# Result rows moved from the GpSimd queue to the SyncE queue in the main loop, and a tail that begins with rounds and runs each gate's conv three ticks behind its loads

## The chip, the cores and the metric

The kernel runs on one core of one Trainium2 chip. The metric is the device time of one execution in microseconds (us), as the median of several runs. The engines are called by the profile's names: PE (TensorE matmul) and PEld (its weight loads), DVE (VectorE), ACT (ScalarE), POOL (GpSimd) and SP (SyncE). SP computes nothing in this kernel, it only issues DMA transfers; POOL computes and also issues transfers of its own.

## What is computed

Two layers work on x of shape (8, 8, 512, 512), each with a residual:

```python
x = x + _L0_conv_ref(_gn(x), ...)     # low modes of a 2-D FFT, mixed over channels, and back
x = x + _L1_conv_ref(_gn(x), ...)     # layer 1, below

# layer 1
grid = drive                           # = x, all 8 channels
for _ in range(15):                    # the map
    mapped = 3.9 * grid * (1.0 - grid)
    local = conv3x3(mapped, K_local, groups=8)
    grid = 0.85 * (0.7 * mapped + 0.3 * local) + 0.15 * drive
cml_out = clip(grid, 0.0001, 0.9999)
nca_out = sigmoid(conv1x1(relu(conv3x3(x, Wp, bp)), Wu, bu))   # 8 -> 128 -> 8
gin = concat([x, cml_out, nca_out])                            # 24 channels
g = sigmoid(conv1x1(relu(conv3x3(gin, Wg1, bg1)), Wg2, bg2))
return g * cml_out + (1.0 - g) * nca_out
```

`_gn` is a group normalisation over pairs of channels. Everything is float32.

## The kernel before

One image of the batch is called an element; there are eight. For each element four kinds of work exist. Their only links are through planes in device memory (xn, the normalised input; cml, the map's result; nca, the result of the hidden branch) and through the order of each engine's instructions.

- **Layer 0** (`layer0`, the spectral pieces) loads x planes of the next element, computes, and writes xn.
- **The map** (`Slabs`, `Tail`, `Phase`) runs 15 steps on slabs of 32 rows that stay in SBUF: `convolve` (192 matmuls in the trace, L524) on PE, `settle` (L537 on DVE, L543 square on ACT), then `renew` (L570, L571), in which POOL issues small transfers that exchange edge rows between slabs. `drive` (L516, on POOL) prepares the summands; `load` (L495, on SP) fetches the slices dE and dO; `leave` stores cml (L600, on SP).
- **The hidden branch** (`Hidden`) works in 128 rounds of four rows per element. `round` makes 24 matmuls in the trace (L723) from a tile "cols", of which two exist; each serves four rounds. When the last round of a tile has been issued (`i == 3`), the tile after the next is requested (`self.load()`, L706, on SP). Every second round a `point` (L742) follows. After every fourth round, the sigmoid result y (L755 on ACT, one buffer) is stored to nca (L758). That is the store of **result rows**. The statement is put off with `later(1, store)` to the end of the tick, and it also sets `e.rows`, the number of rows of nca that gates may read.
- **The gates** (`Gate`) work in 43 blocks of 12 rows per element, on the element before the one that is mapped. `load` issues six transfers on SP (L778 three times: gin from xn, cml and nca; L783 three times: mix). `conv` (L793) follows in a later tick, `point` (L810) in the tick after that, and the output is stored in the next tick by SP (L828), which waits for DVE (L821).

All of this is written out as straight code, and `keep_order` binds each engine to the order of the source. The unit of the order is a **tick** (`turn`, `work`): up to two map steps, then `transfers` (the gates' loads by `others.feed`, and the map's loads), then up to two rounds, then one gate conv (`others.gate`), the hidden point, and one gate point (`others.point`). At the end of a tick the work that was put off is issued. So on SP a tick's gate loads stand ahead of a cols load that the rounds of the same tick request. A cols load that a later tick requests stands behind all of them.

`others.limit` is the number of gates that may be loaded and not yet convolved: two in the main loop, four in the tail. A gate can be convolved when the tick of its loads (`at`) is before the present one.

The last element has no successor. Its map runs with 56 of its 128 rounds (`ROUNDS_LAST`). The other 72 rounds and all 43 of its gates come after the map, in the loop from L1101 on, which is called **the tail** here. (The class `Tail` is something else, the last slab of the map.) In the tail before the change, a quota spreads the 72 rounds evenly over 39 ticks: one in tick 0, one in tick 1, two in most of the later ones. Tick 0 feeds four gates, tick 1 convolves the first of them.

Of the kernel before, what the change touches and what calls it, by code (L numbers as in the profile page):

```python
# [43 lines left out]
N = 512  # L44
# [8 lines left out]
GR = 12  # L53
ROUNDS, ROUNDS_LAST, FIRST_ROUNDS = 128, 56, 8
# [57 lines left out]
def view(t, offset, dims):  # L112

    return bass.AP(tensor=t.tensor, offset=t.offset + offset, ap=[list(d) for d in dims])
# [3 lines left out]
def conv_layers(ctx: ExitStack, tc: tile.TileContext, a, out):  # L118
    nc = tc.nc
# [9 lines left out]
    class Slots:  # L129
# [4 lines left out]
        def __init__(self, most):  # L134
            self.most, self.held = most, {}
# [26 lines left out]
    put_off, now = [], [0]  # L162

    def later(ticks, work):
        put_off.append((now[0] + ticks, work))
# [529 lines left out]
    class Hidden:  # L695
# [42 lines left out]
        def point(self, ps):  # L738

            for r, h in self.hs:  # L740
                for g in range(4):
                    nc.tensor.matmul(  # L742
                        ps[32 * g : 32 * g + 32], w_u[:, r % 4], h[:, g],
                        start=(r == self.hs[0][0]), stop=(r == self.hs[-1][0]),
                        tile_position=(0, 32 * g),
                    )
            if self.hs[0][0] % 4 == 0:
                self.y = wk.tile([P, N], F32, tag="y", name="y", bufs=1)
                nc.scalar.copy(self.y, ps)  # L749
            else:  # L750
                nc.vector.tensor_tensor(self.y, self.y, ps, ALU.add)  # L751
            self.hs.clear()
            if r % 4 == 3:
                y, r0 = self.y, 4 * (r - 3)
                nc.scalar.activation(y, y, AF.Sigmoid, bias=b_u)  # L755

                def store():
                    nc.gpsimd.dma_start(  # L758
                        out=view(self.e.nca, (1 + r0) * C * N, [[N, P], [1, N]]), in_=y
                    )  # L760
                    self.e.rows = r0 + 16

                later(1, store)
# [129 lines left out]
    class Others:  # L893


        def __init__(self):
            self.before, self.after, self.limit = None, None, 2
            self.mapped, self.paused, self.closed = deque(), False, False
            self.loaded, self.convolved, self.pointed = deque(), deque(), deque()
            self.longs = 0  # L900
# [42 lines left out]

        def gate(self, ps):
            self.longs = 0
            if not (self.loaded and self.loaded[0].at < now[0]):
                return False
            g = self.loaded.popleft()
            g.conv(ps)
            g.at = now[0]  # L950
            self.convolved.append(g)
            return True
# [28 lines left out]
    def element(b):  # L981
        e = Element(b)
        phase(e.halves[0])
        phase(e.halves[1] + [e.tail])
        elements.append(e)
        return e

    e = element(0)
# [3 lines left out]
    others = Others()  # L992
# [54 lines left out]
    def turn(at, rounds, e, after, t):  # L1047


        now_phases = [p for p in phases if at < p.end + 2]  # L1050

        def transfers():
            others.feed(t)
            for p in now_phases:
                p.fetch(at)

        def squares():
            for p in now_phases:
                p.squares(at)

        for p in now_phases:
            p.prepare(at)
        steps = [slots[i] for i in (at, at + 1) if 0 <= i < len(slots)]
        work(steps, rounds, e, after and after.hidden, transfers, squares)
# [4 lines left out]
    for b in range(B):  # L1069
        e = elements[b]  # L1070
        after = element(b + 1) if b + 1 < B else None
        others.after = after
        done, rounds = e.hidden.n, ROUNDS if after else ROUNDS_LAST
        first, second = phases[2 * b : 2 * b + 2]
        ticks = (second.end - at + 1) // 2
# [8 lines left out]
        for t in range(ticks):  # L1084
# [7 lines left out]
            more = done + quota[t] - e.hidden.n  # L1092
# [5 lines left out]
        others.mapped.append(e)  # L1098


    others.after, others.limit, others.paused, others.closed = None, 4, False, False  # L1101
    shared.most = SLOTS
    done, ticks = e.hidden.n, -(-N // GR) - 4
    for t in count():
        if e.hidden.n == ROUNDS and not others.mapped and not others.busy():
            break
        more = min(ROUNDS, done + (t + 1) * (ROUNDS - done) // ticks) - e.hidden.n
        turn(at, min(more, 2 - e.hidden.n % 2), e, None, GATES_FROM)
        at += 2
    tick(end=True)  # L1110
# [55 lines left out]
```

## Time and profile before

| what | value |
|---|---|
| median of 3 runs | 9497.11 us (9489.37 to 9503.13) |
| the profiled execution | time 9518.56 us, span 9516.7 us from first to last instruction |
| PE busy | 9080.2 us, 95% of the span |
| ACT, DVE, POOL busy | 4072.7, 5655.6, 3505.6 us |
| result stores L758 on POOL | 256, mean some 0.62 us of issue, 3.7 us to landing (median) |
| idle time of POOL before L758, waiting for y (ACT L755) | 373.5 us, 72 times |
| the map's last matmul (L524) ends | 9052 us |
| the tail, to the end of the span | from 9058 to 9516.7 us |

How to read it: the profiled execution is one single execution and slower than the median of the runs by some 21 us, so a sum of its parts is compared with its own time, and only differences are carried over to the median. A time in square brackets on a line of the timeline is the idle time of that engine before the instruction, with what ended it. A name like `gin<-nca` says what is written from what. "SPq" is SP's queue of DMA issues. The line of an issue gives only the time of issuing; when a transfer lands is seen from who waits for it.

### The profile page before, as it was taken

How to read it: one execution, taken by the hardware profiler on the slowest of the kernel's cores; microseconds unless marked ns; L12 is line 12 of the kernel's file. 1: busy time of each engine (PE TensorE's matmuls, PEld its weight loads, DVE VectorE, ACT ScalarE, POOL GpSimd, SP SyncE). 2: the span in 40 equal slices, each digit the busy share in tenths (PEclk: the TensorE clock that was granted, in tenths of full speed). 3: DMA queues.
4: the chain of work that ended last, by engine and by line, in shares of the span. 5: the costliest groups of instructions: out<-in, count | busy, mean ns of one | idle time of the engine just before them, and what ended most of it. 6: DMA issues, size and time to landing. Idle time of an engine off the chain costs nothing. (4 is left out here: it accounts for less than half of the span.)

```text
span 9516.7 us, 331665 instructions
## 1 busy us (share of the span) xinstructions
PE 9080.2 (95%) x148976; PEld 4064.1 (43%) x148976; DVE 5655.6 (59%) x5820; ACT 4072.7 (43%) x4285; POOL 3505.6 (37%) x4678
## 2 busy tenths in 40 slices
PE   6999999999999999999999999999999999999989
PEld 3444444444444444444444444444444444334433
DVE  5665566655666556665566555665556655555555
ACT  2444444444444444444344444444444444334422
POOL 3242434334343343433434333343433434343422
PEclk9999999999999999999999999999999999999999
DMA  4241365565655656655556556565565555565488
GB/s 150 83 127 35 94 170 131 144 145 136 156 134 146 139 133 154 162 137 139 136 143 160 137 126 157 128 164 138 125 161 138 160 135 119 142 151 126 104 210 201
DMA packets 682173, 1327.07 MB, mean 139 GB/s; under 512 B 146938, under 2 KB 152442, under 8 KB 653266
## 3 DMA queue, kind: packets, MB, share of 16 engines
q1 hardware_dynamic: 557568, 1181.97, 49.9%
q0 software_dynamic: 120832, 122.73, 4.8%
q8 instruction: 1171, 19.19, 0.9%
q14 instruction: 248, 2.03, 0.1%
q10 hardware_dynamic: 2354, 1.14, 0.0%
HBM read 977.48 MB, written 270.61 MB: 131 GB/s over the span
## 5 line engine op out<-in xcount | busy, mean ns | idle before, releaser
L524 PE MATMUL pair<-m,band 32*32 32x512 f32 x103680 | 3722.9, 605 | 184.6 <-issue 123.5
L543 ACT ACTIVATE m<-m 128x1024 f32<-128x1024 f32 x2016 | 2125.9, 1055 | 2500.1 <-DVE m L537 2419.2
L723 PE MATMUL pair<-cols,w_p 32*128 32x511 f32 (+1 forms) x24576 | 2867.6, 605 | 44.6 <-DVE m L537 20.9
L524 PEld LDWEIGHTS pair<-m,band 32*32 32x32 f32 x103680 | 1994.1, 103 | 1837.9 <-issue 1082.2
L570 POOL DMA_DIRECT2D m<-m x1568 | 862.7, 550 | 3591.7 <-ACT m L543 3519.7
L537 DVE SCALAR_TENSOR_TENSOR m<-pair,dO 128x1024 f32<-128x1024 f32 x1152 | 1356.2, 1219 | 1183.2 <-PE pair L524 1031.0
L723 PEld LDWEIGHTS pair<-cols,w_p 32*128 32x128 f32 x24576 | 1305.2, 187 | 1628.3 <-issue 1164.4
L537 DVE SCALAR_TENSOR_TENSOR m<-pair,dE 128x1024 f32<-128x1024 f32 x1008 | 1187.3, 1219 | 1105.3 <-PE pair L524 940.1
L731 DVE TENSOR_SCALAR h<-pair,b_p 128x1024 f32<-128x1024 f32 x1024 | 1311.2, 1282 | 868.5 <-PE pair L723 863.6
L729 ACT ACTIVATE h<-pair,b_p 128x1024 f32<-128x1024 f32 x1024 | 1140.4, 1114 | 916.8 <-PE pair L723 916.7
L742 PE MATMUL pair<-h,w_u 128*32 128x512 f32 x8192 | 1059.1, 610 | 34.5 <-ACT h L729 30.5
L793 PE MATMUL pair<-gin,w_g 128*32 128x511 f32 (+1 forms) x8256 | 963.4, 598 | 35.4 <-DMA gin<-nca 31.8
L816 POOL TENSOR_TENSOR mix<-mix 96x512 f32<-96x512 f32 x344 | 438.4, 1274 | 1273.8 <-ACT mix L814 1233.7
L571 POOL DMA_DIRECT2D m<-m x1568 | 844.1, 538 | 26.6 <-issue 23.2
L742 PEld LDWEIGHTS pair<-h,w_u 128*32 128x32 f32 x8192 | 245.4, 110 | 691.3 <-issue 353.6
L755 ACT ACTIVATE y<-y,b_u 128x512 f32<-128x512 f32 x256 | 184.8, 722 | 831.0 <-DVE y L751 831.0
L793 PEld LDWEIGHTS pair<-gin,w_g 128*32 128x32 f32 x8256 | 235.2, 110 | 713.0 <-issue 490.2
L798 POOL TENSOR_TENSOR mix<-mix 96x512 f32<-96x512 f32 x344 | 445.3, 1294 | 51.2 <-DMA mix<-cml 28.5
L547 POOL TENSOR_SCALAR dO<-dO 128x2048 f32<-128x2048 f32 x72 | 391.7, 5440 | 99.1 <-DVE m L537 98.0
L749 ACT COPY y<-pair 128x512 f32<-128x512 f32 x256 | 150.0, 586 | 646.0 <-PE pair L742 522.7
L821 DVE SCALAR_TENSOR_TENSOR mix<-mix,back 96x512 f32<-96x512 f32 x344 | 334.9, 974 | 143.9 <-POOL mix L816 143.9
L803 DVE TENSOR_SCALAR mix<-pair,b_g 128x512 f32<-128x512 f32 x344 | 257.7, 749 | 201.5 <-PE pair L793 200.3
(90 smaller groups left out, 3430.8 us busy)
## 6 DMA issues: line engine op xcount, KB each, us to landing
gin<-xn SPq DMA_DIRECT2D x344, 384.0 KB
cols<-xn SPq DMA_DIRECT2D x256, 512.0 KB
x<-in_x SPq DMA_DIRECT2D x120, 1024.0 KB
gin<-cml SPq DMA_DIRECT2D x344, 320.0 KB
gin<-nca SPq DMA_DIRECT2D x344, 320.0 KB
dE<-xn SPq DMA_DIRECT2D x288, 256.0 KB
dO<-xn SPq DMA_DIRECT2D x288, 256.0 KB
mix<-xn SPq DMA_DIRECT2D x344, 192.0 KB
```

Of the source, the lines that this page charges most:

```text
L524: nc.tensor.matmul(ps[h // 2][32 * t : 32 * t + 32, h % 2], band[at, self.channel(step - 1, h, t), dx], m[at, t, dx : dx + N], start=(n == ...
L537: nc.vector.scalar_tensor_tensor(u[:, at], ps[q], FLOOR, d[:, at], ALU.max, ALU.add)
L543: nc.scalar.square(u[:, at], u[:, at])
L570: nc.gpsimd.dma_start(out=view(tb, rb, dims), in_=view(ta, ra, dims))
L571: nc.gpsimd.dma_start(out=view(ta, ra + s, dims), in_=view(tb, rb + s, dims))
L723: nc.tensor.matmul(ps[g // 2][:, g % 2, lo:hi], w_p[p, dx, i % 2], self.cols[p, i // 2, at : at + hi - lo], start=(n == 0), stop=(n == 2), ...
L729: nc.scalar.activation(h[:, :2], ps[0], AF.Relu, bias=b_p)
L731: nc.vector.tensor_scalar(h[:, 2:], ps[1], b_p, 0.0, ALU.add, ALU.max)
L742: nc.tensor.matmul(ps[32 * g : 32 * g + 32], w_u[:, r % 4], h[:, g], start=(r == self.hs[0][0]), stop=(r == self.hs[-1][0]), tile_position ...
L793: nc.tensor.matmul(ps[32 * j : 32 * j + 32, lo:hi], gband[:, dx], gin[:, j, at : at + hi - lo], start=(n == 0), stop=(n == 2), tile_positi ...
L798: nc.gpsimd.tensor_tensor(d, d, ng, ALU.subtract)
L816: nc.gpsimd.tensor_tensor(d, d, mix[: GR * C, 2], ALU.mult)
```

## The change

The change has three parts.

1. The result store L758 is issued by SP instead of POOL as long as `others.lag` is 0, which is the whole time before the tail; in the tail POOL issues it as before. The last store ahead of the tail belongs to the first group.
2. A new number `others.lag` is 0 in the main loop and 2 in the tail. A gate can be convolved when `at + lag` is before the present tick: in the tail three ticks after its loads instead of one.
3. The tail's quota begins with two rounds in each of ticks 0 to 3. The 64 others are spread evenly over ticks 4 to 40 (before: all 72 over ticks 0 to 38). Since a tick takes no more than two rounds, and one after an odd number, five pairs of ticks with a single round each remain (before: two such pairs, apart from ticks 0 and 1).

The first gate's conv so moves from tick 1 to tick 3, the last one's from tick 43 to tick 45. The number of instructions of every kind stays the same.

```diff
                 def store():
-                    nc.gpsimd.dma_start(
+                    (nc.gpsimd if others.lag else nc.sync).dma_start(
                         out=view(self.e.nca, (1 + r0) * C * N, [[N, P], [1, N]]), in_=y
                     )
                     self.e.rows = r0 + 16
...
-            self.before, self.after, self.limit = None, None, 2
+            self.before, self.after, self.limit, self.lag = None, None, 2, 0
...
-            if not (self.loaded and self.loaded[0].at < now[0]):
+            if not (self.loaded and self.loaded[0].at + self.lag < now[0]):
                 return False
...
-    others.after, others.limit, others.paused, others.closed = None, 4, False, False
+    others.after, others.limit, others.lag = None, 4, 2
+    others.paused, others.closed = False, False
     shared.most = SLOTS
-    done, ticks = e.hidden.n, -(-N // GR) - 4
+    done, ticks = e.hidden.n, -(-N // GR) - 2
     for t in count():
         if e.hidden.n == ROUNDS and not others.mapped and not others.busy():
             break
-        more = min(ROUNDS, done + (t + 1) * (ROUNDS - done) // ticks) - e.hidden.n
+        more = min(ROUNDS, done + 8 + (t - 3) * (ROUNDS - done - 8) // (ticks - 4)) - e.hidden.n
+        if t < 4:
+            more = 2
         turn(at, min(more, 2 - e.hidden.n % 2), e, None, GATES_FROM)
```

## The prediction

> **What bounds the kernel now.** I read the page's busy table first, then busy time by stretch over the whole span, then the timeline of the last 480 us, then the waits. The busy table says which engine to follow.
>
> ```profile
> PE 9080.2 (95%) x148976; PEld 4064.1 (43%) x148976; DVE 5655.6 (59%) x5820; ACT 4072.7 (43%) x4285; POOL 3505.6 (37%) x4678
> ```
>
> PE is busy 95% of 9516.7 us. By stretch (length, busy us of PE, PEld, DVE, ACT and POOL, clock, DMA share, GB/s) the end reads:
>
> ```profile
> 9042.00:9093.00 51.00, 27.00 (x350) 10.67 (x344) 18.89 (x17) 5.18 (x5) 2.34 (x2) 0.77 0.70 173
> 9093.00:9478.00 385.00, 385.00 (x3405) 137.00 (x3404) 223.73 (x200) 124.53 (x144) 104.33 (x94) 1.00 0.88 218
> 9478.00:9517.00 39.00, 15.49 (x112) 4.01 (x105) 14.63 (x16) 3.42 (x5) 14.09 (x10) 0.83 0.52 129
> ```
>
> The tail's middle is PE without a gap; its start holds one hole. The timeline shows the hole and what SP does in it:
>
> ```profile
> 9058.34 5.43 PE L723 MATMUL pair<-cols,w_p 32*128 32x512 f32 x48
> 9064.38 8.32 SPq L778 DMA_DIRECT2D gin<-xn  x1
> 9087.05 4.53 PE L793 MATMUL pair<-gin,w_g 128*32 128x512 f32 x24 [23.28 <-DMA gin<-nca]
> 9104.80 0.32 SPq L778 DMA_DIRECT2D gin<-xn  x1
> 9112.47 0.38 SPq L706 DMA_DIRECT2D cols<-xn  x1
> 9115.29 0.32 SPq L778 DMA_DIRECT2D gin<-xn  x1
> ```
>
> PE runs two rounds, then idles 23.28 us until the first gate's loads land. SP issues four gates' loads (24 transfers) from 9064.38 to 9104.42, then gate 5's, and only then, at 9112.47, the next rows for the rounds (cols). For the main loop the waits matter (total us, times, longest):
>
> ```profile
> POOL nca L758 <- ACT y L755: 373.5, 72, 28.5
> SPq L828 <- DVE mix L821: 3294.1, 303, 29.4
> ACT y L749 <- DMA nca<-y: 59.4, 14, 5.3
> ```
>
> POOL stands in front of the result store; SP has much idle time; the one buffer y is hardly ever late (13 of those 14 waits are in the tail).
>
> **What the Trainium skill says.** "DMA: Bandwidth & Descriptors", section Queues, rings and completion order: a sequencer's DMA is split over rings of its own row, and each DMA engine consumes a ring in order. The trace agrees: SP lets a transfer go when the one eight places before it has landed (gate 6's first load goes at 9115.29, as gate 5's first, issued 9104.80, lands), so landings keep nearly the order of issue. The same page, section Issuing engines are not separate DMA queues: another issuing engine saves only the issue time. The trace gives that time, 0.62 us a store on POOL. "TensorE: Matmul & The Clock Gate", section Part 1: The HAM clock gate: after an idle window the array runs at half rate. Agreed: granted clock 0.50 from 9068 to 9086, and the gate conv after the hole takes 4.53 us where later ones take 2.78.
>
> **The tail, step by step.** A full tick (two rounds, their point, a gate's conv and point) repeats every 10.63 us (9093.23, 9103.86 and on). Two ticks of one round each take 14.41 (9210.19 to 9224.60): one gate more, so a gate costs 3.78 and two rounds with their point 6.85. Two rounds and point without a gate take 7.84 (164.90 to 172.74 to 180.58 at the kernel's start), since the point then waits for h.
> Before: the tick of rounds 58 and 59 starts at 9093.23. From there 70 rounds (35 x 6.85) and 37 gates (37 x 3.78) give 9472.9; the last round's tick does end at 9473.0. The remaining 43.8 us, five gates that wait for loads, are alike after the change: there too gates 39 to 43 remain when rounds end, and gate 42 waits for the last store.
> After: ticks 0 to 3 run rounds 56 to 63. They take 3 x 7.84, then 6.85 plus gate 1's conv 2.78: 9058.34 + 33.2 = 9091.5. Gate 1's loads landed at 9087, so its conv no longer waits. The 23.3 us hole is filled.
> **What is late next:** tick 4 begins with round 64, whose cols tile is loaded when round 59 is issued, in tick 1. But tick 0's feed has put four gates' loads ahead of it in SP's queue. It can take gate 5's place, 9104.80. That place landed after 10.5 us; the cols transfer of before (512 KB) took 11.1, its landing read from the store that SP lets go eight transfers later. So 9115.6, plus about 1.2 us since two result stores of 256 KB now fall before it and only one did (256 KB at 218 GB/s). PE resumes at 9117 after 25 idle us, cold: the first two rounds at 141.8 took 8.32 instead of 5.43, a cold gate conv 1.75 more; I take 2.3. Then 64 rounds (32 x 6.85 = 219.2) and 37 gates (139.9): 9478.4. Against 9472.9 the tail is **5.5 us longer**. One hole has replaced another of the same size. Bounds: if cols were in time, 9091.5 + 359.1 = 9450.6, -22; if it lands at 9121, as late as the slowest nearby transfer (13 us), +10.
> The later single rounds of the new schedule (five pairs of ticks instead of two) cost no PE work. They need loads sooner: 359.1/37 = 9.7 us a gate; gates 2 to 6 landed every 7.8 to 9.6, so they are covered, by 12 to 17 us of slack between landing and conv in steady state.
>
> **The stores in the main loop.** 237 of 256 stores lie before 9042, and they plus one more go to SP.
> *Off POOL:* 237 x 0.62 = 147 us of issue and 558 us of standing. Behind a store stands next a renewal (L570) in 165 cases, always with a gap, since it waits for ACT's square of the next tick, later in ACT's order than y; removing the store does nothing there. In 44 cases drives (L516) or L547 follow at once, 20 of these chains hold a renewal, and all PE waits on m<-m at a matmul sum to 28.4 us. I take -3 us; bounds 0 and -20.
> *Onto SP:* 237 x 0.62 us. Matching each store's place in program order to SP's transfers: in 189 places SP sits idle across it. In 48 the next transfers move back, together 141 us, of which 131 in 30 places, at most 7.6. Queued behind it are dE/dO slices, x planes and gate loads; after each such run SP idles 7 to 29 us, so no delay is carried on. At 2834.5 the dO slices land 7.6 late, 2852; the drive (2.7) ends 2855, its reader starts 2858.8: hidden. At 2367.4 a gate's loads land 6 late, about 2390, when its conv starts (2390.19): just covered. I take +2; bounds 0 and +44 (a third of 131).
> *The buffer y:* a store on SP's rings lands behind loads of up to 14 us, where POOL's took 3.6 in the middle. In 16 places it would land after the next copy (L749) wants y, together 42 us; ACT idles some 3.8 us before its next square, which covers most. I take +2; bounds 0 and +20.
>
> **Sum.** +5.5 - 3 + 2 + 2 = +6.5 us. The profiled execution has span 9516.7 and time 9518.6, 21.5 above the median 9497.1; the difference carries over: 9497.1 + 6.5 = 9503.6, told as **9503**.
>
> **Rivals.**
> A, the forecast (0.61): hole for hole, main loop neutral; 9503, own range 9489 to 9516. For it: the queue order and the landing times.
> B, the hole is really filled (0.19): cols lands in time, or POOL's relief is worth its bound; -22 - 3 gives 9472, and part of it up to 9485. Against it: 24 transfers of 6.4 MB stand ahead, from 9072.7 on, and at the tail's 218 GB/s they need 30 us, till 9103.
> C, slower (0.20): the store at the head of SP's queue waits for y and holds dE/dO and gate loads whose landing PE needs; a third of 131 us plus the tail's 5.5 gives 9546. It decides as soon as the slack between a load's landing and its reader is under the delay, as it nearly is at 2390. Half of its weight lies under 9530.
> The change not doing what it says is not likely: the lag only delays convs that are ready, but tick 1 to 3 have rounds in their place.
>
> **How the numbers follow.** What a measurement tells from no change is about 0.2%, 19 us: faster is below 9478, slower above 9516. B gives faster 0.19, C slower 0.20, A the same 0.61. The range 9474 to 9530 holds A, most of B and half of C; it takes in the tail's bounds (-22, +10) and most of the main loop's.
>
> **What would show it.** Right: no wait at the first L793 of the tail; a PE wait on cols<-xn of 22 to 28 us before round 64; cold matmuls after it; the tail from 9058 to the last round's end 3 to 8 us longer; L758 on SP, POOL's wait on L755 gone but in the tail; PE idle from 400 to 9042 within 15 us of the 300 us that busy time by stretch gives there. Wrong: round 64 starting near 9092; PE waits on dO, gin or m<-m in the main loop growing by over 20 us.

## The result and the profile after

| kernel | runs | median, us | ratio to before, 95% interval |
|---|---|---|---|
| before | 6 | 9505.62 (9489.37 to 9530.28) | |
| changed | 6 | 9443.68 (9431.73 to 9457.31) | 0.9932 [0.9916, 0.9949] |
| changed, once more, beside the last experiments | 6 | 9440.28 (9422.39 to 9465.90) | 0.9945 [0.9925, 0.9965] |

The change is worth 0.55 to 0.7%, 52 to 65 us. The forecast was 9503, no change. The page of the changed kernel, for comparison with the busy table of before:

```profile
span 9440.3 us, 331607 instructions
PE 9039.4 (96%) x148976; PEld 4068.9 (43%) x148976; DVE 5657.6 (60%) x5820; ACT 4072.3 (43%) x4285; POOL 3367.1 (36%) x4440
q0 software_dynamic: 101792, 60.33, 3.1%
q8 instruction: 1171, 19.19, 0.9%
```

POOL has lost 238 instructions: the stores are gone from it. PE has as many instructions as before but is busy 41 us less, so its matmuls ran at full clock for longer. The line q8 (packets, MB, share of 16 engines) was passed over in the prediction; it becomes the main point below.

**The tail grew.** From its first round to the end of the span it took 9516.7 - 9058.34 = 458.4 us before and 9440.3 - 8974.16 = 466.1 after: 7.7 us more; to the end of the last round, which is what the forecast of 5.5 us sums, it is 415.2 against 425.5 us, 10.3 more (the second trace of the changed kernel, experiment 12, has 420.2, 5.0 more). The timeline of the changed kernel's tail:

```profile
8974.16 5.43 PE L723 MATMUL pair<-cols,w_p 32*128 32x512 f32 x48
8978.59 7.74 SPq L758 DMA_DIRECT2D nca<-y  x1
8995.73 0.58 ACT L749 COPY y<-pair 128x512 f32<-128x512 f32 x1 [14.94 <-DMA nca<-y]
8996.37 4.46 PE L723 MATMUL pair<-cols,w_p 32*128 32x512 f32 x24 [11.45 <-ACT y L749]
9016.46 2.78 PE L793 MATMUL pair<-gin,w_g 128*32 128x512 f32 x24
9020.36 1.01 SPq L706 DMA_DIRECT2D cols<-xn  x2
9032.81 5.01 PE L723 MATMUL pair<-cols,w_p 32*128 32x512 f32 x24 [11.86 <-DMA cols<-xn]
9355.06 6.89 PE L723 MATMUL pair<-cols,w_p 32*128 32x512 f32 x48 [3.17 <-DMA cols<-xn]
```

The first gate's conv (9016.46) no longer waits. In place of its 23.28 us there are two waits, 11.45 and 11.86. The second is the forecast one, for cols behind 24 gate loads. The first wasn't foreseen: the last store before the tail still goes to SP, stands there behind the cml stores, and holds the one buffer y. PE comes 11 us later to round 64, so it waits so much less there: the forecast's 25 us are the sum, 23.3, in two pieces. A third wait, of 3.17 us at 9355.06, is again for cols; the forecast had none there.

**The gain lies in the main loop.** Between the first and the last convolve (L524) before took 8871.5 us and after 8784.0, 87.5 less. By stretch (length, busy us of PE, PEld, DVE, ACT, POOL, clock, DMA share, GB/s), first of before, then of after:

```profile
400.00:9042.00 8642.00, 8341.87 (x140604) 3757.86 (x140581) 5150.76 (x5217) 3801.03 (x3970) 3263.57 (x4314) 0.98 0.55 137
```

```profile
400.00:8960.00 8560.00, 8297.28 (x140688) 3764.14 (x140672) 5158.45 (x5218) 3799.86 (x3970) 3130.82 (x4085) 0.99 0.56 138
```

PE's idle time falls from 300.1 to 262.7 us and its clock rises. The waits say which idle time. Of before (us in total, times, longest):

```profile
PE pair L524 <- issue: 123.5, 79, 4.1
PE pair L524 <- DMA m<-m: 28.4, 17, 3.8
```

Of after, with SP's wait at the store and the y buffer:

```profile
PE pair L524 <- issue: 103.3, 69, 3.9
PE pair L524 <- DMA m<-m: 22.7, 13, 4.2
SPq L758 <- ACT y L755: 922.1, 187, 10.1
ACT y L749 <- DMA nca<-y: 44.9, 10, 14.9
```

The largest loss on PE has no releaser ("issue"), and it shrinks. SP now stands 922 us before the store, and no group of PE's waits in the main loop of this trace is longer by more than 4.2 us. Of ACT's 44.9 us for y, 2.6 lie in the main loop (at 2345.0 and 6943.3), the rest in the tail.

### The profile page after: what moved, and what is told of

It is laid out like the page before. It is cut to its first block, busy times and chain, and to the rows that moved or that the text cites. A ratio compares the mean times of both kernels' runs of the same rounds, so it can differ in the third digit from the quotient of the medians.

```text
span 9440.3 us, 331607 instructions
## 1 busy us (share of the span) xinstructions
PE 9039.4 (96%) x148976; PEld 4068.9 (43%) x148976; DVE 5657.6 (60%) x5820; ACT 4072.3 (43%) x4285; POOL 3367.1 (36%) x4440
## 3 DMA queue, kind: packets, MB, share of 16 engines
q8 instruction: 1171, 19.19, 0.9%
## 5 line engine op out<-in xcount | busy, mean ns | idle before, releaser
L524 PE MATMUL pair<-m,band 32*32 32x512 f32 x103680 | 3703.2, 604 | 159.3 <-issue 103.3
L524 PEld LDWEIGHTS pair<-m,band 32*32 32x32 f32 x103680 | 1997.7, 103 | 1788.1 <-issue 997.9
L793 PE MATMUL pair<-gin,w_g 128*32 128x511 f32 (+1 forms) x8256 | 962.2, 598 | 11.3 <-DMA gin<-nca 7.9
L793 PEld LDWEIGHTS pair<-gin,w_g 128*32 128x32 f32 x8256 | 235.3, 110 | 686.8 <-issue 462.9
L516 POOL TENSOR_SCALAR dO<-dO,base 128x512 f32<-128x512 f32 x288 | 208.8, 735 | 574.6 <-DMA dO<-xn 532.7
```

Source lines behind the costliest of these rows:

```text
L524: nc.tensor.matmul(ps[h // 2][32 * t : 32 * t + 32, h % 2], band[at, self.channel(step - 1, h, t), dx], m[at, t, dx : dx + N], start=(n == ...
L793: nc.tensor.matmul(ps[32 * j : 32 * j + 32, lo:hi], gband[:, dx], gin[:, j, at : at + hi - lo], start=(n == 0), stop=(n == 2), tile_positi ...
```

## What "issue" is: the place at 2371 us

The convolve that starts at 2371.11 before starts at 2361.62 after. Before:

```profile
2366.84 0.38 SPq L706 DMA_DIRECT2D cols<-xn  x1
2367.40 0.33 SPq L778 DMA_DIRECT2D gin<-xn  x1
2369.55 0.44 SPq L783 DMA_DIRECT2D mix<-nca  x1
2371.11 5.76 PE L524 MATMUL pair<-m,band 32*32 32x512 f32 x167
2371.99 0.36 SPq L182 DMA_DIRECT2D x<-in_x  x1
2373.05 0.60 POOL L758 DMA_DIRECT2D nca<-y  x1 [2.87 <-ACT y L755]
2380.98 2.00 PE L524 MATMUL pair<-m,band 32*32 32x512 f32 x25 [4.10 <-issue]
```

After:

```profile
2357.35 0.38 SPq L706 DMA_DIRECT2D cols<-xn  x1
2361.62 6.58 PE L524 MATMUL pair<-m,band 32*32 32x512 f32 x192
2363.23 0.33 SPq L758 DMA_DIRECT2D nca<-y  x1
2363.73 0.51 SPq L778 DMA_DIRECT2D gin<-xn  x1
2366.08 0.42 SPq L783 DMA_DIRECT2D mix<-nca  x1
2368.13 5.43 PE L723 MATMUL pair<-cols,w_p 32*128 32x512 f32 x48
```

Before, SP issues a gate's six loads from 2367.40 on, ahead of the convolve. The convolve stops after 167 of its 192 matmuls for 4.10 us, and the profile names nothing that it waited for. In the changed kernel the store stands in front of those loads on SP and waits for y; the loads leave 6 us later relative to PE's work, and the convolve runs through.

What PE waits for is in the trace's DMA records: the queue q8 carries packets of 16 KB, 1171 in all, one for some 254 of PE's 297,952 instructions (19.19 MB in the page). The Trainium skill ("Advanced Engine Details and Errata", section ISA Cache) says that instructions are cached in lines of 16 KB, 256 instructions; the packets agree. What follows is read from these records; no line of the page has it. At this place the packet that follows the convolve's start begins 1.1 us after it in the changed kernel and 6.8 us after it before; it takes 1.1 to 1.3 us, and PE resumes 1.8 us after it has landed. What the DMA engines moved between the convolve's start and the packet's shows why SP's wait matters here (length, busy us of PE, PEld, DVE, ACT, POOL, clock, DMA share, GB/s), of before and of after:

```profile
2371.11:2377.89 6.78, 5.77 (x171) 3.25 (x167) 3.24 (x4) 2.70 (x3) 0.60 (x1) 1.00 1.07 191
```

```profile
2361.62:2362.74 1.12, 1.12 (x40) 0.50 (x39) 0.83 (x2) 0.26 (x1) 0.00 (x0) 1.00 0.06 22
```

Before, 191 GB/s go on for 6.78 us until the packet begins; after, SP stands at the store, the data pause at 22 GB/s, and the packet begins in the pause.

The same pattern of late packets is found all over the main loop: from 400 us on, before had 58 gaps of over 0.6 us ahead of L524 without a releaser, 115.1 us together. All 58 end 1.23 to 1.78 us after such a packet has landed (median 1.42), and in the 4 us before them the core's DMA moved 222 GB/s (median), against 137 over the stretch. PE waits for its own instructions, which come late in bursts of loads. A burst is needed, but isn't enough: of the 1107 such packets from 400 us to the last convolve of before, 566 began when less than 160 GB/s had landed in the 4 us ahead, and none of them was followed (1 to 2 us after it landed) by a stop of PE over 0.6 us without a releaser; of the 443 that began after 190 GB/s or more, 60 were. What makes these 60 late and not the others is not shown.

A stop costs twice. The Trainium skill ("TensorE: Matmul & The Clock Gate", Part 1) says that the array's clock is halved after at least one idle window of about 3.4 us. Here shorter stops were followed by half clock too: of the 65 stretches at a granted clock of 0.5 in the main loop of before, 51 had no single gap as long as that from 8 us ahead of their start to 4 us behind it. Half of PE's busy time in such stretches, which is what the slow clock costs, is 143.6 us before and 102.6 (54 stretches) after. The 87.5 us so divide into gaps 37.6 (304.7 to 267.1), cold clock (time lost to half clock) 41.0, and 9 of the rest. By what ended the gap, with each cold stretch put down to the longest gap near its start: the late instructions 20.2 of gap and 14.6 of cold clock; the spectral matmuls L428 waiting for h 15.1 and 13.3; m<-m 5.7 and 6.5. L428's wait for h varies from trace to trace (17.1 us before, 6.1 in experiment 2 with the same main loop), so its part can't be credited to the change.

One trace is not enough for such a sum: the kernel with the tail alone changed (below) has the main loop of before, and its trace shows 8839.5 us there, 32 less, and 125.0 us of cold clock instead of 143.6. So the following compares medians, and the idle time before L524 over many traces.

## The experiments

Theories. **S**: SP is held at the store, so bursts of loads leave later and PE's instructions come through. **P**: POOL is relieved of standing and issuing. **R**: all of it is a chance shift of collisions. Later **P2**, a form of P: only the earlier departure of the rows counts. Ratios are to before, run on the same chip. In the edits, `others.tail` is a flag that is set where the tail begins, and `seen` is a scratch row in device memory; lines below an edit have shifted numbers in that run's views (L793 becomes L795, and so on).

**1. The store alone.** The choice of engine for L758 of the changed kernel, lag and quota as before.

```diff
-                    nc.gpsimd.dma_start(
+                    (nc.gpsimd if others.tail else nc.sync).dma_start(
```

> The store alone: SP issues it while the map runs, POOL in the tail; the tail's lag and quota are those of before. If the whole gain comes from the main loop (theories S, P and R below alike), the main loop gives some -70 us and the tail, now that of before, gives back the 7.7 us that it grew: about 9430 us against 9505. If the prediction's account of the store (+1 us) were right and the gain came from elsewhere, it is 9500 to 9510.

Measured 9436.96 us, 0.9922 [0.9907, 0.9937]: the whole gain is the store's.

**2. The tail alone.** The changed kernel with `nc.gpsimd.dma_start` for every store.

> The tail alone: lag and new quota as in the changed kernel, every store on POOL. Its main loop is that of before, so it is also a second trace of that. The prediction's own tail sum gives +5.5 us, with one wait of 22 to 28 us for the cols tile: about 9511 us. If the tail were where the gain came from, it lies under 9480.

Measured 9512.93 us, 1.0004 [0.9993, 1.0015]. The wait for cols is there at the size that the prediction gave, and late in the tail a second one:

```profile
9084.45 4.76 PE L723 MATMUL pair<-cols,w_p 32*128 32x512 f32 x24 [22.18 <-DMA cols<-xn]
9410.44 8.17 PE L723 MATMUL pair<-cols,w_p 32*128 32x512 f32 x48 [5.70 <-DMA cols<-xn]
```

So lag and quota together win nothing; in this trace the time from the last convolve to the end is 479.2 us against 464.6 of before, in the changed kernel's 472.4. Six traces with the tail of before (before, 1, 3, 4, 5, 8) have 458.8 to 468.4 us, so the new tail alone is some 10 to 20 us longer in this trace; the medians of the times differ by 9 us, within the noise of the ratio.

**3. The store on ACT.** As 1, with `nc.scalar` for `nc.sync`.

> As the store alone, but ACT issues the store in the main loop, so POOL is relieved and SP is neither held nor given anything. Theory P (the gain comes from POOL, which no longer stands before the store and moves its small exchanges sooner): main loop -60 to -80 us, less some 10 us for 238 issues on ACT, about 9435 to 9445. Theory S (the gain comes from SP, which waits for y at the store and so puts off the bursts of loads queued behind it): no gain, 9495 to 9515. Theory R (chance shift of collisions): anything between.

Measured 9470.60 us, 0.9961 [0.9947, 0.9975].

**4. SP waits, POOL stores.**

```diff
                     self.e.rows = r0 + 16
+                    if not others.tail:
+                        nc.sync.dma_start(out=seen, in_=y[:1, :16])
```

> The kernel before, store left on POOL; at the store's place SP in addition writes 64 bytes of y to a scratch row, so that SP waits for y as in the changed kernel but moves no rows. Theory S: most of the gain of the main loop, -50 to -80 us, about 9430 to 9455. Theory P: no gain, 9500 to 9515, POOL stands before the store as ever. Theory R: anything between.

Measured 9467.61 us, 0.9955 [0.9940, 0.9970]. Neither S nor P alone: each gives about half, -36 and -33 us, and the sum, -69, is what the store alone gave (-67), though nothing here shows that the two parts add. The trace of 4 at the place above has SP's wait in the same spot and no gap, with the store still on POOL:

```profile
2358.76 6.58 PE L524 MATMUL pair<-m,band 32*32 32x512 f32 x192
2360.38 0.23 SPq L763 DMA_DIRECT2D seen<-y  x1
2360.65 0.60 POOL L758 DMA_DIRECT2D nca<-y  x1 [2.86 <-ACT y L755]
2360.79 0.33 SPq L780 DMA_DIRECT2D gin<-xn  x1
```

The traces show the first half plainly. From the first to the last convolve the kernels in which SP isn't held take 8871.5, 8839.5, 8837.0 and 8860.5 us (before, 2, 3, 5); those in which it is held at the store's place take 8805.5, 8803.3, 8784.0, 8771.8, 8807.1 and 8803.2 (1, 4, changed twice, 6, 8). They don't show the second half: 4 and 8, where POOL still stands, are longer than the changed kernel's two but no longer than 1 and 6, and single executions of one kernel scatter by 10 us and more. POOL's part rests on the times alone.

R as the whole story falls at single places, too: the time from this convolve's start to the next one's is 25.6, 25.6, 19.2 and 20.7 us in the four traces in which SP isn't held (before, 2, 5, 3), and 18.3 in each of the six in which it is (1, 4, 6, 7, 8, changed). At 6388 us of before it is 16.6 to 21.4 against 14.6, at 6914 us 17.4 to 19.2 against 14.3 to 14.4.

**5 and 8. POOL made to stand again.** To 3 (as 5) and to 1 (as 8) this is added:

```diff
+                    if not others.tail:
+                        nc.gpsimd.dma_start(out=seen, in_=y[:1, :16])
```

> The store issued by ACT in the main loop, and POOL at the store's place in addition writes 64 bytes of y to a scratch row: POOL stands and issues as before, the rows travel from ACT. The store on ACT alone gained 33 us. If that was POOL's standing and issuing (theory P as first put), it is lost here: 9495 to 9510 us. If it is that the rows leave earlier than POOL got to them, so that the loads behind them land earlier too (theory P2), it stays: 9465 to 9480.

Measured 9500.58 us, 0.9999 [0.9987, 1.0011].

> The store alone on SP (9437 us), and POOL in addition writes 64 bytes of y at the same place, so that it stands and issues as before. Theory P: its half of the gain is lost, about 9470 us. Theory P2: nothing is lost, 9432 to 9445.

Measured 9448.87 us, 0.9942 [0.9930, 0.9954]. With the rows on ACT all of the gain is lost (30 us by the medians), so it was POOL's standing and issuing, not the rows' departure; what POOL's 64-byte transfer costs of itself was not measured apart. With the rows on SP 12 us are lost by the medians and 19 by the ratios, between what P and P2 said, and the intervals of 1 and 8 overlap. Off POOL is worth 12 to 33 us, by what it is combined with. How it reaches PE is only partly seen. PE's wait for m<-m at L524 has a mean of 30.8 us over the five traces in which POOL stands (before, 2, 4, 5, 8) and 25.1 over five in which it doesn't (1, 3, 6, 7, changed). That is 6 us of gap with some cold clock. Through what else POOL reaches PE stays open.

**6. The tail mended.** Aimed at the two waits of the changed kernel's tail:

```diff
-                    (nc.gpsimd if others.lag else nc.sync).dma_start(
+                    (nc.gpsimd if others.lag or others.after is None and self.n >= ROUNDS_LAST else nc.sync).dma_start(
...
+        others.limit = 2 if t < 2 else 4
         turn(at, min(more, 2 - e.hidden.n % 2), e, None, GATES_FROM)
```

> The changed kernel with two edits in the tail: the last store of the map's rounds goes to POOL, and only two gates may be loaded in ticks 0 and 1 of the tail, four from then on. If the two waits of 11.4 us (for y) and 11.9 us (for cols) in the changed kernel's tail come from that store's place on SP and from the 24 gate loads ahead of cols, both go: about 23 us under the changed kernel, some 9420 us. If the gates loaded two ticks later then come late, half of it or nothing is left.

Measured 9431.73 us, 0.9924 [0.9911, 0.9936]. The tail, from the last convolve on, is 445.9 us in its trace, against 472.4 and 466.3 in the two traces of the changed kernel. The wait for y is down to 0.89 us and the one for cols to 5.95 us, half of what it was; 12 gate loads still stand ahead of that tile.

```profile
9023.50 2.85 PE L723 MATMUL pair<-cols,w_p 32*128 32x512 f32 x24 [0.89 <-ACT y L749]
9036.73 5.50 PE L723 MATMUL pair<-cols,w_p 32*128 32x512 f32 x24 [5.95 <-DMA cols<-xn]
```

The median moved by 12 us only, less than the tail's 20 to 26; the interval of the ratio is about as wide as the difference. In the pair 7 and 9 below the same edit gives about what the tail says.

**7. SP held in each tick.** To the changed kernel:

```diff
                 later(1, store)
+            elif not others.lag:
+                mark = wk.tile([1, 16], F32, tag="mark", name="mark", bufs=1)
+                nc.scalar.copy(mark, self.y[:1, :16])
+                later(1, lambda: nc.sync.dma_start(out=seen, in_=mark))
```

> The changed kernel, with SP also held in those ticks that store no rows: it writes 64 bytes to a scratch row that wait for ACT's copy of y (through a small copy of their own). Theory S: the loads that stand behind leave PE's instruction fetch its turn in these ticks too, another -20 to -36 us: 9405 to 9425. If the gain of S is bound to few places or the delay of the loads costs as much, it is at 9435 to 9460.

Measured 9415.74 us, 0.9905 [0.9892, 0.9918]: 28 us under the changed kernel, from transfers that carry nothing. Held more often, SP gives more, as S says. The page's groups of this kernel (busy, mean ns | idle before, of it without releaser):

```profile
L524 PE MATMUL pair<-m,band 32*32 32x512 f32 x103680 | 3687.4, 604 | 130.7 <-issue 73.4
```

**9. Held in each tick, tail mended.** The edits of 6 and 7 together.

> The changed kernel with SP held in each tick of the main loop and with both edits in the tail. Held each tick it took 9416 us; its tail still has the waits of 11.8 and 12.3 us. The mended tail measured 445.9 us in its trace against 472.4. If the two add up: about 9392 us. If the mended tail is worth only the 12 us that lie between the medians of the mended and the changed kernel: 9404.

Measured 9385.13 us, 0.9881 [0.9862, 0.9901]. Against 7 the mended tail is worth 0.0024 of 9500, 23 us: the tails of 472.3 and 448.3 us in the two traces say the same. The median lies below both of the values expected, and the intervals of 7 and 9 overlap a little, so the trace is the better evidence for this step.

**10. Loads in halves, nothing else.** The kernel before, stores on POOL; in `Gate.load`, between the gin and the mix loads:

```diff
+            if not others.tail:
+                nc.sync.dma_start(out=seen, in_=self.gin[88:89, 0, :16])
```

> The kernel before, stores on POOL; only, in the main loop, between the three gin and the three mix loads of a gate SP writes 64 bytes of gin to a scratch row, so it waits until gin has landed and never has more than half of a gate's loads under way. Nothing of the store is changed. Theory S (bursts of loads keep PE's instruction fetch waiting): the idle time of PE before L524 without a named releaser falls from some 118 us to below 100, time 9465 to 9490. Rival (the store's place is what matters, not the bursts): no gain or, since loads land later, a loss: 9500 to 9530.

Measured 9407.91 us, 0.9900 [0.9882, 0.9919]: 0.01 of 9500, 95 us (91 by the medians), more than the change, without touching a store. The gain is far larger than S expected here (9465 to 9490 us), so the expectation had its sign and not its size. The store's place on SP is thus not needed: holding the loads is. The waits of this kernel:

```profile
PE pair L524 <- issue: 70.9, 45, 3.6
PE pair L524 <- DMA m<-m: 15.2, 10, 3.9
PE pair L795 <- DMA gin<-nca: 25.1, 2, 23.2
PE pair L812 <- DVE mix L805: 10.7, 23, 2.8
```

The wait for m<-m falls too (28.4 to 15.2), as it would if the bursts also delayed POOL's small exchanges; that was not tested. Holding SP makes gates late only a little: of the 25.1 us of their convs, 23.2 are the old hole at the head of the tail, and their points (L812, L810 in before) wait for DVE 10.7 us instead of 3.4.

What the holds do to the bursts differs. In the main loop of before, 38% of all 4 us pieces move more than 190 GB/s. With SP held at the store's place or in each tick it is 37 to 39%, and 434 to 460 instruction packets begin in such bursts (before 443); but 38 to 55 of them are followed by a stop of PE, where before had 60. So these holds don't make the bursts fewer, they move them. With the gate loads in halves the bursts themselves are fewer: 30% of the pieces, 369 packets, 41 stops.

**11. Held in each tick, mended, and in halves.** The edits of 6, 7 and 10.

> SP held in each tick, mended tail, and gate loads in halves in the main loop. Theory S: the idle time of PE before L524 without a releaser falls under the 73 us of the version held each tick, and time under that of the held and mended version by 5 to 25 us. If the holds already do what can be done, or the gates' loads come late: the same time or up to 20 us more.

Measured 9374.26 us, 0.9868 [0.9849, 0.9888], the lowest median of all: 124 us under before and 66 under the changed kernel (12). The 11 us to experiment 9 are within the intervals, which overlap.

```profile
L524 PE MATMUL pair<-m,band 32*32 32x512 f32 x103680 | 3654.6, 601 | 108.4 <-issue 54.4
```

**12. The changed kernel again**, beside these.

> The changed kernel once more, on the same chip as the versions built on it: 9435 to 9450 us. Its main loop is that of the store alone (9437 us with the old, shorter tail), and its tail's two waits should be there again.

Measured 9440.28 us; waits of 10.80 and 10.29 us in the tail. Set side by side, the idle time before L524 without a releaser orders the kernels by how SP is held (one trace each; the first two rows come within 3 us of each other):

| SP's loads | idle before L524 without releaser, us |
|---|---|
| not held (before, 2, 3, 5) | 123.5, 115.9, 121.2, 109.8 |
| held in every second tick (changed twice, 1, 4, 6, 8) | 103.3, 89.6, 95.3, 95.5, 107.3, 101.0 |
| held in each tick (7, 9) | 73.4, 80.1 |
| gate loads in halves (10) | 70.9 |
| both (11) | 54.4 |

## Why the prediction was wrong, step by step

- *The tail, hole for hole, +5.5 us.* Right in mechanism; in size 5 to 14 us. To the end of the last round it grew by 10.3 and 5.0 us in the two traces of the changed kernel and by 13.6 with the tail alone changed (428.8 against 415.2), two of these at or beyond the bound of +10. With the tail alone, the cols wait was 22.18 us (forecast 25) and the conv's wait gone. Missed were the last store on SP, which splits the wait in two, and a late wait for cols (3.17 and 5.70 us), where the step asked only whether the gates' loads come in time.
- *Off POOL, -3 us, bounds 0 and -20.* Right in sign, mis-sized: 12 to 33 us. The step counted only PE's waits for m<-m, of which 6 us go in the mean; it put everything else that POOL's standing may cost at nothing. What that is stays open.
- *Onto SP, +2 us, bounds 0 and +44.* **This is the step that failed.** It asked only whom a later load could hurt, found that nearly none was late, and set the lower bound at nothing. By itself SP's wait is worth -36 us (experiment 4), and with all of the store off POOL the main loop gave about -67 (experiment 1) where the three terms for the stores came to +1. The displaced loads, 48 runs of them, were rightly found; that their going later takes them out of the way of something else wasn't considered. The loss without a releaser, 123.5 us, the largest of PE's, was on the page and left unexplained.
- *The buffer y, +2 us.* Right for the main loop; ACT's wait for it there is 2.6 us in the trace after, as small as before (2.9). In the tail, the one store on SP ahead of it costs 14.94.
- *The rivals.* B (9472, the hole really filled) had the right side by luck: its tail gain didn't come, and POOL's relief alone isn't the gain. C (PE waits for loads held on SP) didn't occur: no wait of PE for dO, gin or m<-m grew by 20 us. None of the three had the mechanism that decided.
- *The signs named.* No wait at the first L793, cold matmuls after the cols wait (5.01 us for a round that takes 2.85 warm), L758 on SP: as said. The tail to the last round's end, said to be 3 to 8 us longer, was 10.3 longer in the first trace and 5.0 in the second. The cols wait of 22 to 28 us holds for the tail alone and not for the changed kernel. PE's idle time in the main loop, said to stay within 15 us of 300, fell to 262.7: that one showed the error.

## What to carry to other kernels

Idle time of PE without a releaser is a cost with a cause: look for what lands just before it ends, and count the cold clock after it. A wait put ahead of loads that have slack can be a gain: here it moved bursts off instruction packets or, placed between a gate's loads, made them fewer. So the range for "the loads go later" has to reach below nothing. A queue that a store leaves and one that it enters are tested apart by a transfer of 64 bytes at the same place.

## What was not expected of the hardware

- PE's instructions travel as packets of 16 KB among the data (1171 packets, 19.19 MB). Such a packet takes about 1.1 us (median of before), and most are in time. At three places (2371, 6388 and 6914 us of before) it began 5 to 7 us after the convolve's start instead of 1.0 to 2.4 (the same places with SP held at the store), and PE then stood for 2 to 4 us.
- The Trainium skill ("DMA: Bandwidth & Descriptors", section Queues, rings and completion order) says that a DMA engine serves its queues in turn, a packet at a time. That alone doesn't tell why one packet comes so late, and no run here shows the turns; whether the packet is asked for late or held stays open.
- PE's gaps cost about half as much again in clock: 143.6 us lost to half clock beside 304.7 us of gaps in the main loop of before. Gaps of 2 us were enough for it: at 2769 us one of 2.32 us was followed by 3.4 us at half clock.
